# Layer 2 attention: the step loop's instructions in source order instead of a scheduler's, and the block end's rstd one piece later

## The chip, the cores and the metric

The kernel runs on one core of one Trainium2 chip, in float32 throughout. The metric is the device time of one execution in microseconds (us), lower being better. The profile is of one execution, taken by the hardware profiler; engines are named as its page names them: PE (matmul), PEld (weight load), DVE (VectorE), ACT (ScalarE), POOL (GpSimd), SP (the queue that issues most DMAs).

## The reference, cut to what matters

The program is a network of four layers on an image of 2 x 64 x 64 positions with 128 channels. Only the attention of layer 2 is touched here. It sees the image as 2 sequences (batches) of L = 4096 tokens; `t` is the residual, `_ln_t` a layer norm without weights.

```python
q = silu(x @ Wq + bq); k = silu(x @ Wk + bk); v = silu(x @ Wv + bv)
u = x @ Wu + bu                                   # 256 wide
pos_attn = einsum('nm,bmd->bnd', rel, v)          # rel is a Toeplitz matrix of pos_w
scores = einsum('bhnd,bhmd->bhnm', qh, kh) / sqrt(hd)     # 4 heads of 32
scores = where(causal, scores * scores, 0.0)
self_attn = einsum('bhnm,bhmd->bhnd', silu(scores), vh)
a = concatenate([self_attn, pos_attn], axis=-1)
a = (a - mean(a)) * rsqrt(var(a) + 1e-3) * ln_gamma + ln_beta
out = relu(u * a @ Wf + bf) + x
t = t + out                                       # x here is _ln_t(t)
```

There is no softmax: a score is squared, masked by causality and put through Silu.

## The kernel before

The kernel is written on a layer that tracks tiles and dependences. After the program is traced, a scheduler decides in which order each engine gets its instructions, by a cost model of its own; each engine then takes its queue strictly in that order, and semaphores hold an instruction until its inputs are there and its output buffer is free. The order in the source is therefore only a wish unless a region is marked as scheduled by hand.

`layer2_attn` first loads and prepares weights: the Toeplitz table `toe` (L1042 and L1043), the folded weights `wuy` and `buy` (`l2_folded`). The two sequences are then cut into 16 blocks of 512 queries, in the order 7, 0, 6, 1, 5, 2, 4, 3 for each batch, a long one and a short one in turn, since by causality block `qb` has `4 * qb + 4` tiles of 128 keys. The innermost unit is a *step*: one block and one key tile. There are 288 steps. The last four steps of each block are diagonal: they are masked by `tri`, and have 512, 384, 256 and 128 live query columns.

One step, in source order, does this. `scores` (L1301) multiplies the four heads, two heads a pair, into two score tiles of 128 x 1024 in PSUM; the pool holds two such tiles, so each is overwritten by the next step. The first pair goes to ACT, which squares it into an `es` tile (L1315), and on a diagonal step DVE masks that tile (L1318). The second pair goes to DVE, which scales it (L1328, with L1324 for the masked part), and POOL multiplies it by itself (L1331). Then come `silu(at - 1, 2)`, the Silu (L1338) of the first pair of the step before, `silu(at - 2, 3)`, the Silu of the second pair of two steps before, and `values(at - 3)` (L1352), the product of scores and values of three steps before, summed in one PSUM bank `av` over the block. At a block's end `av` is copied to `selfT` (L1363).

All other work of the layer is written as generators, cut into *pieces* by `yield`, in a table of jobs with a number of pieces each; after each step as many pieces are run as make the table finish in time (`left`, `due`). A piece may also be forced earlier, by `finish`, where something needs it. The jobs:

- `norm_stats`: the statistics (L1089, L1090) of a batch's 32 token tiles, and their rstd.
- `keys`: `transposed` (four normalises on DVE, L153, four transposes on PE, L1108, a copy on DVE, L1110, and for some an add on POOL, L1113), the key projection and its Silu (L1125, L1126), the value projection, its add and its Silu (L1130, L1138, L1141).
- `prepare`: the same `transposed` for the queries of the next block, the query projection and its Silu (L1180, L1181), and the projection `u`, four matmuls and adds (L1187, L1190). Before its first piece it finishes the output of three blocks before.
- `rest`: sums of the values on DVE (L1150), a matmul and a copy.
- `positions`: the Toeplitz product (L1202), one group of four matmuls for a key tile, then an add (L1214).
- `join`: transposes of `selfT` (L1229), a copy into `a` (L1232), the layer norm's statistics and rstd (`ln_stats`), and four products with `u` (L1236).
- `output`: eight transposes (L1251), two copies (L1252), sixteen matmul records (L1258), four multiply-adds that use the rstd (L1268), and the residual add (L1274).

The rstd (`rstd`) is one add on DVE (L95), one Sqrt on ACT (L97) and four small operations on DVE (L99 to L103). [...] ACT loads a table before and after. All the small PSUM tiles of these jobs share one tag, `misc`, with two buffers.

Of the kernel before, what the change touches and what calls it, by code (L numbers as in the profile page):

```python
# [8 lines left out]
F32 = mybir.dt.float32  # L9
# [5 lines left out]
P = 128  # L15
# [23 lines left out]
class Net:  # L39
# [969 lines left out]
    def layer2_attn(self):  # L1009
# [3 lines left out]
        nc, tc, ins = self.nc, self.tc, self.ins  # L1013
        pos_w = ins["L2_attn_pos_rev"]
        with ExitStack() as st:
# [46 lines left out]
            queries, cats, selfs, rs = {}, {}, {}, {}  # L1062
            jobs = {}

            def add(key, pieces, gen, first=False):
                if first:
                    rest = dict(jobs)
                    jobs.clear()
                    jobs[key] = [pieces, gen]
                    jobs.update(rest)  # L1070
                else:
                    jobs[key] = [pieces, gen]
# [7 lines left out]
            def finish(key):  # L1080
                while key in jobs:
                    piece(key)


            def norm_stats(b):
                mv = self.small.tile([P, NC, 2], F32, tag="l2mv", name=f"l2mv{b}", bufs=2)
                for n in range(NC):
                    s6 = self.small.tile([P, 6], F32, tag="lst", name=f"l2st{b}_{n}")
                    nc.vector.bn_stats(s6, self.x[:, b * NC + n, :])  # L1089
                    nc.vector.bn_aggr(mv[:, n, :], s6)  # L1090
                    if n % 4 == 3:
                        yield
                r = self.small.tile([P, NC], F32, tag="l2r", name=f"l2rs{b}", bufs=2)
                self.rstd(r, mv[:, :, 1], 1e-5, NC)
                kTs[b] = {}
                vs[b] = ap.tile([P, NC, C], F32, tag="v", name=f"l2v{b}")
                stats[b] = mv, r
# [18 lines left out]
            def keys(b, g, add_back=False):  # L1116
                finish(("stats", b))
                v = vs[b]
                slot = g if b == 0 else (8 + g if g < 4 else 11 - g)
                kT = ap.tile([P, 512], F32, tag=f"kT{slot}", name=f"l2kT{b}_{g}", bufs=1)  # L1120
                kTs[b][g] = kT
                xT = transposed(b, g, "k", add_back)
                yield
                pk = ps.tile([P, 512], F32, tag="misc", name=f"l2pk{b}_{g}")
                nc.tensor.matmul(pk, lhsT=wk, rhs=xT, start=True, stop=True)  # L1125
                nc.scalar.activation(kT, pk, AF.Silu, bias=bk)  # L1126
                yield
                pv = ps.tile([P, 4, C], F32, tag="misc", name=f"l2pv{b}_{g}")
                for i in range(4):
                    nc.tensor.matmul(  # L1130
                        pv[:, i, :],
                        lhsT=xT[:, i * P : (i + 1) * P],
                        rhs=wv,
                        start=True,
                        stop=True,
                    )
                part = v[:, 4 * g : 4 * g + 4, :]
                nc.vector.tensor_tensor(  # L1138
                    part, pv, bv.unsqueeze(1).broadcast_to([P, 4, C]), ALU.add
                )  # L1140
                nc.scalar.activation(part, part, AF.Silu)  # L1141
                yield
# [78 lines left out]
            def join(b, qb, i):  # L1221

                finish(("prepare", i))
                finish(("pos", i))
                a, u = cats[i], queries[i][1]
                t = f"{b}_{qb}"
                pt = ps.tile([P, 4, C], F32, tag="misc", name=f"l2st{t}")
                for j in range(4):
                    nc.tensor.transpose(  # L1229
                        pt[:, j, :], selfs[i][:, j * P : (j + 1) * P], self.ident  # L1230
                    )
                nc.vector.tensor_copy(a[:, :, :C], pt)  # L1232
                mv, r = self.ln_stats(a, 4, 1e-3, f"l2o{t}")
                rs[i] = r
                for j in range(4):
                    nc.vector.scalar_tensor_tensor(  # L1236
                        a[:, j, :], a[:, j, :], mv[:, j, 0:1], u[:, j, : 2 * C],
                        ALU.subtract, ALU.mult,
                    )
                yield  # L1240
                yield

            def output(b, qb, i):
                finish(("join", i))
                a = cats[i]
                t = f"{b}_{qb}"
                aT = ap.tile([P, 2, 512], F32, tag="aT", name=f"l2aT{t}", bufs=1)
                for k in range(2):
                    pa = ps.tile([P, 4, P], F32, tag="misc", name=f"l2pa{t}_{k}")
                    for j in range(4):  # L1250
                        nc.tensor.transpose(pa[:, j, :], a[:, j, k * C : (k + 1) * C], self.ident)  # L1251
                    nc.vector.tensor_copy(aT[:, k, :], pa.rearrange("p i q -> p (i q)"))  # L1252
                    yield
                yield
                po = ps.tile([P, 4, C], F32, tag="misc", name=f"l2po{t}")
                for j in range(4):
                    for k in range(2):
                        nc.tensor.matmul(  # L1258
                            po[:, j, :],
                            lhsT=aT[:, k, j * P : (j + 1) * P],  # L1260
                            rhs=wf[:, k, :],
                            start=(k == 0),
                            stop=(k == 1),
                        )
                o = ap.tile([P, 4, C], F32, tag="o", name=f"l2o{t}", bufs=1)
                y = queries[i][1]
                for j in range(4):
                    nc.vector.scalar_tensor_tensor(  # L1268
                        o[:, j, :], po[:, j, :], rs[i][:, j : j + 1], y[:, j, 2 * C :],
                        ALU.mult, ALU.add,  # L1270
                    )
                n0 = b * NC + 4 * qb
                xs = self.x[:, n0 : n0 + 4, :].rearrange("p i c -> p (i c)")
                nc.vector.scalar_tensor_tensor(  # L1274
                    xs, o.rearrange("p i c -> p (i c)"), 0.0, xs, ALU.max, ALU.add
                )
                yield
# [64 lines left out]
            def values(at):  # L1342
                if not 0 <= at < len(steps):
                    return
                (i, k, off), es = steps[at][:2]
                b, qb = order[i]
                last = k == 4 * qb + 3
                if k == 0:
                    avs[i] = ps.tile([P, 512], F32, tag="av", name=f"l2av{b}_{qb}", bufs=1)
                for h in range(NH):  # L1350
                    hs = slice(h * HD, (h + 1) * HD)
                    nc.tensor.matmul(  # L1352
                        avs[i][hs, off:],
                        lhsT=vs[b][:, k, hs],
                        rhs=es[h // 2][:, h % 2, off:],
                        start=(k == 0),
                        stop=last,
                    )
                if last:
                    if i >= 2:  # L1360
                        finish(("join", i - 2))
                    selfs[i] = ap.tile([P, 512], F32, tag="selfT", name=f"l2sT{b}_{qb}")
                    nc.vector.tensor_copy(selfs[i], avs[i])  # L1363
                    add(("join", i), 2, join(b, qb, i))
                    add(("out", i), 4, output(b, qb, i))

            add(("stats", 0), 8, norm_stats(0))
            add(("keys", 0, 0), 3, keys(0, 0))
            add(("prepare", 0), 4, prepare(0, 7, 0, add_back=False))
# [516 lines left out]
```

## Time and profile before

| what | value |
|---|---|
| time, median of 3 runs | 5103.84 us (5092.13 to 5111.22) |
| the profiled execution | 5117.86 us |
| its span, first to last instruction | 5116.1 us |
| mean granted TensorE clock | 0.901 |
| busy: PE, PEld, DVE | 89%, 40%, 56% of the span |
| busy: ACT, POOL | 47%, 12% of the span |
| layer 2 attention, first Square to last | 2173.2 to 3397.0 us |
| busy from 2300 to 2500 us: PE, DVE, ACT, POOL | 182.29, 97.73, 130.67, 76.88 of 200 us |

How to read it: busy time is the union of an engine's instructions. A line of the waits names an engine, a line of the source and a tile, what ended the wait, then the total in us, the number of waits and the longest. A line of a timeline has start and length in us, engine, line, operation, output and inputs, shapes and the count of instructions merged into it; in brackets stands the idle time of that engine just before, and what ended it. Each float32 matmul of the source shows as two records.

### The profile page before, as it was taken

What the parts mean: (1) busy time and instruction counts of PE and PEld (TensorE: products, weight loads), DVE (VectorE), ACT (ScalarE), POOL (GpSimd) and SP (SyncE); (2) the same over time, 40 slices, a digit from 0 to 9 for tenths busy, and PEclk for the clock granted to TensorE, in tenths of its full rate; (3) what the DMA queues carried; (4) which work ended last, traced back from release to release, by engine and by line L of the source; (5) the groups of instructions that cost most, each with busy time, mean ns of one, the idle gap of its engine ahead of it and who ended that gap; (6) DMA issues with size and microseconds to landing.
All of it is one profiled execution on the core that took longest, in us unless ns stands there. A gap on an engine that the chain in (4) does not pass through costs nothing.

```text
span 5116.1 us, 69030 instructions
## 1 busy us (share of the span) xinstructions
PE 4573.2 (89%) x28099; PEld 2063.1 (40%) x28099; DVE 2866.2 (56%) x4880; ACT 2396.9 (47%) x2773; POOL 637.6 (12%) x386
## 2 busy tenths in 40 slices
PE   7999999999999958499889988876999999999766
PEld 6433333443333326333322222224985444444432
DVE  2567777667787788854544454453032333333477
ACT  3556666655666625176666777741013222222200
POOL 1000000000000020144334444420001000000000
PEclk7899999999999978699899999975559999999889
DMA  4232323332333300000000000020410000000000
GB/s 125 66 60 47 59 63 75 81 75 57 61 53 55 61 10 1 24 1 1 1 1 1 1 1 1 1 69 26 123 51 1 0 0 0 0 1 0 5 11 24
DMA packets 132798, 164.96 MB, mean 32 GB/s; under 512 B 13904, under 2 KB 76208, under 8 KB 131568
## 3 DMA queue, kind: packets, MB, share of 16 engines
q1 hardware_dynamic: 110560, 143.25, 13.1%
q10 hardware_dynamic: 21904, 17.12, 1.1%
q8 instruction: 225, 3.69, 0.3%
q14 instruction: 109, 0.89, 0.1%
HBM read 130.97 MB, written 29.36 MB: 31 GB/s over the span
## 4 chain that ended last, share of the span: by engine, by line
PE 74%; DVE 14%; ACT 6%; POOL 4%; issue 2%; DMA 1%; SPq 0%; DVEq 0%; POOLq 0%; ACTq 0%
PE l0sc L592 18%; PE l0o L546 9%; PE scl L1650 9%; PE oTl L1667 9%; PE l2sc L1301 4%; POOL l2es L1331 3%; PE f3ex L1824 2%; ACT l2es L1338 2%; PE l2pos L1202 2%; DVE l2es L1328 2%; PE f2po L1528 2%; PE l2av L1352 2%; PE f2ph L1502 2%; ACT l2es L1315 2%; DVE l0acc L614 2%; PE l0pw L405 2%
## 5 line engine op out<-in xcount | busy, mean ns | idle before, releaser
L614 DVE TENSOR_TENSOR l0acc<-l0acc,l0es 128x1024 f32<-128x1024 f32 x988 | 1210.0, 1225 | 540.9 <-PE l0o L546 377.4
L606 ACT ACTIVATE l0es<-l0sc 128x1024 f32<-128x1024 f32 x992 | 940.3, 1031 | 387.2 <-PE l0sc L592 386.3
L592 PE MATMUL l0sc<-l0mv,ka 64*64 64x512 f32 x8192 | 993.4, 617 | 18.8 <-ACT l0es L606 16.5
L1338 ACT ACTIVATE l2es<-l2es 128x1024 f32<-128x1024 f32 (+3 forms) x576 | 562.0, 984 | 256.8 <-POOL l2es L1331 220.5
L1675 DVE TENSOR_TENSOR accl<-accl,esl 128x1024 f32<-128x1024 f32 x240 | 294.1, 1225 | 540.7 <-ACT esl L1661 482.9
L1331 POOL TENSOR_TENSOR l2es<-l2es 128x1024 f32<-128x1024 f32 (+3 forms) x288 | 504.1, 1750 | 726.6 <-DVE l2es L1328 662.9
L592 PEld LDWEIGHTS l0sc<-l0mv,ka 64*64 64x64 f32 x8192 | 297.8, 136 | 624.3 <-issue 378.5
L1661 ACT ACTIVATE esl<-scl 128x1024 f32<-128x1024 f32 x240 | 245.5, 1023 | 550.8 <-PE scl L1650 550.8
L1328 DVE TENSOR_SCALAR l2es<-l2sc 128x1024 f32<-128x1024 f32 (+3 forms) x272 | 306.8, 1128 | 341.3 <-PE l2sc L1301 341.1
L546 PE MATMUL l0o<-l0es,l0v 128*32 128x512 f32 x3968 | 495.0, 602 | 0.0
L1301 PE MATMUL l2sc<-l2q,l2kT 32*128 32x512 f32 (+3 forms) x2304 | 405.0, 623 | 91.1 <-ACT l2es L1315 67.7
L1650 PE MATMUL scl<-l3qT,l3kT 128*128 128x512 f32 x1024 | 484.1, 595 | 1.8 <-DVE bok_l L246 1.8
L1667 PE MATMUL oTl<-esl,l3v 128*128 128x512 f32 x960 | 448.5, 592 | 0.0
L1352 PE MATMUL l2av<-l2es,l2v 128*32 128x512 f32 (+3 forms) x2304 | 308.3, 603 | 0.0
L1315 ACT ACTIVATE l2es<-l2sc 128x1024 f32<-128x1024 f32 (+3 forms) x288 | 269.6, 936 | 53.6 <-PE l2sc L1301 53.2
L1650 PEld LDWEIGHTS scl<-l3qT,l3kT 128*128 128x128 f32 x1024 | 192.8, 191 | 233.2 <-issue 218.6
L1202 PE MATMUL l2pos<-l2v,toe 128*32 128x512 f32 (+3 forms) x2304 | 277.2, 572 | 0.0
L1667 PEld LDWEIGHTS oTl<-esl,l3v 128*128 128x128 f32 x960 | 182.4, 190 | 229.6 <-issue 225.8
L1301 PEld LDWEIGHTS l2sc<-l2q,l2kT 32*128 32x128 f32 x2304 | 122.8, 189 | 336.3 <-ACT l2es L1315 217.5
L868 POOL TENSOR_TENSOR l1y<-l1y,l1gb 128x1024 f32<-128x1024 f32 x8 | 20.3, 2532 | 1861.8 <-DVE l1y L862 1842.7
L546 PEld LDWEIGHTS l0o<-l0es,l0v 128*32 128x32 f32 x3968 | 106.9, 109 | 337.8 <-issue 337.8
L1832 DVE SCALAR_TENSOR_TENSOR x<-f3ex,f3wt,x 128x128 f32<-128x128 f32 x512 | 160.2, 347 | 28.5 <-PE f3ex L1824 20.0
(438 smaller groups left out, 4265.0 us busy)
## 6 DMA issues: line engine op xcount, KB each, us to landing
l0mv<-l0qd SPq DMA_DIRECT2D x128, 256.0 KB, 7.6
l0mv<-l0hd SPq DMA_DIRECT2D x256, 128.0 KB, 6.5
l0mv<-l0wd SPq DMA_DIRECT2D x128, 128.0 KB, 5.6
l0wd<-l0rw SPq DMA_DIRECT2D x4, 2048.0 KB, 6.8
l0hd<-l0hst SPq DMA_DIRECT2D x32, 256.0 KB, 2.1
f2w<-in_L_ffn_weight_dram ACTq DMA_DIRECT2D x32, 256.0 KB, 10.9
f2w<-in_L_ffn_weight_dram ACTq DMA_DIRECT2D x8, 1024.0 KB, 4.9
f2w<-in_L_ffn_weight_dram SPq DMA_DIRECT2D x8, 1024.0 KB
```

The source lines that it names most:

```text
L546: nc.tensor.matmul(o[0][at : at + HD, :], lhsT=v[:, 2 * j + s, HD * h : HD * (h + 1)], rhs=es[s][:, h, :], start=(j == 0), stop=(j == NX * ...
L592: nc.tensor.matmul(sc[64 * c : 64 * c + 64, h, :], lhsT=ka[rows, k0 : k0 + 64], rhs=mv[rows, yb, :], start=True, stop=True,)
L606: nc.scalar.activation(es, sc, AF.Exp)
L614: nc.vector.tensor_tensor(entry[5], entry[5], es, ALU.add)
L1202: nc.tensor.matmul(pos[c : c + 32, j0:, :], lhsT=toe[:, d * P + c : d * P + c + 32], rhs=v[:, n0 + j0 - d : n0 + 4 - d, :], start=(d == 0) ...
L1301: nc.tensor.matmul(sc[:, h2, off:], lhsT=kT[hs, cols], rhs=q[hs, off:], start=True, stop=True,)
L1328: nc.vector.tensor_scalar(es[:, :, lo:], sc[:, :, lo:], root, None, ALU.mult)
L1331: nc.gpsimd.tensor_tensor(part, part, part, ALU.mult)
L1338: nc.scalar.activation(e[:, :, off:], e[:, :, off:], AF.Silu)
L1352: nc.tensor.matmul(avs[i][hs, off:], lhsT=vs[b][:, k, hs], rhs=es[h // 2][:, h % 2, off:], start=(k == 0), stop=last,)
L1650: nc.tensor.matmul(sc[:, i, :], lhsT=kT[:, k * P : (k + 1) * P], rhs=qs, start=True, stop=True,)
L1667: nc.tensor.matmul(oT, lhsT=v[:, k, :], rhs=es[:, i, :], start=(k == 0), stop=(k == NC - 1),)
```

## The change

Two edits. From the point where the first jobs are added, the rest of `layer2_attn` is put under `tc.manual_schedule()`: inside it each engine receives its instructions in the order in which the source issues them. The region ends with the function. And in `join` the call of `ln_stats` is written out: the statistics come before the four products as they did, but the rstd is called after the first `yield`, so in `join`'s second piece, which was empty.

```diff
@@ in join
-                mv, r = self.ln_stats(a, 4, 1e-3, f"l2o{t}")
-                rs[i] = r
+                mv = self.small.tile([P, 4, 2], F32, tag="lmv4", name=f"mv_l2o{t}")
+                for j in range(4):
+                    s6 = self.small.tile([P, 6], F32, tag="lst", name=f"st_l2o{t}{j}")
+                    nc.vector.bn_stats(s6, a[:, j, :])
+                    nc.vector.bn_aggr(mv[:, j, :], s6)
                 for j in range(4):
                     nc.vector.scalar_tensor_tensor(
                         a[:, j, :], a[:, j, :], mv[:, j, 0:1], u[:, j, : 2 * C],
                         ALU.subtract, ALU.mult,
                     )
                 yield
+                rs[i] = self.small.tile([P, 4], F32, tag="lr4", name=f"r_l2o{t}")
+                self.rstd(rs[i], mv[:, :, 1], 1e-3, 4)
                 yield
@@ ahead of the first jobs
+            st.enter_context(tc.manual_schedule())
             add(("stats", 0), 8, norm_stats(0))
             add(("keys", 0, 0), 3, keys(0, 0))
             add(("prepare", 0), 4, prepare(0, 7, 0, add_back=False))
```

How the built programs' instructions stand shows what this moves. Before, the scheduler had put each first-pair Silu directly behind its own Square in ACT's queue, and the second pair's Silu of the same step behind that, in most steps; after, the queue is Square of a step, first-pair Silu of the step before, second-pair Silu of two steps before. PE's queue had values three steps late already and keeps that. Before, the transposes, output matmuls and query projections of a block's end were spread over the scores of the next three steps; after, transposes, output matmuls and the transposes for the next queries stand in one row between the first and the second step's scores in blocks 2 to 8 and 10 to 14 (counted from 0), in nine of these twelve with the query projection as well, and DVE's part of them likewise. Before, the statistics of batch 1 stood ahead of the loop; after, they stand in steps 14 to 18 of the first block, with a pair of table loads of their own. The other layers' instructions and SP's queue keep their order.

## The prediction

> **What bounds the kernel now.** I read the page first (groups of instructions), then the waits inside the layer-2 attention (2130 to 3440 us), then its timeline. Layer 2 attention runs from the first Square at 2173.2 us to the last at 3397.0: 1224 us for 288 steps, 24% of the span. Nothing outside it is edited. On the page two groups stand out, ACT's Silu and POOL's multiply:
>
> ```profile
> L1338 ACT ACTIVATE l2es<-l2es 128x1024 f32<-128x1024 f32 (+3 forms) x576 | 562.0, 984 | 256.8 <-POOL l2es L1331 220.5
> L1331 POOL TENSOR_TENSOR l2es<-l2es 128x1024 f32<-128x1024 f32 (+3 forms) x288 | 504.1, 1750 | 726.6 <-DVE l2es L1328 662.9
> ```
>
> After the bar is the idle time before the group and what ended it: ACT stood 220.5 us waiting for POOL. The waits give the rest:
>
> ```profile
> ACT l2es L1338 <- POOL l2es L1331: 220.5, 205, 4.2
> PEld l2sc L1301 <- ACT l2es L1315: 217.5, 179, 2.9
> ...
> DVE l2es L1318 <- ACT l2es L1315: 177.4, 61, 4.3
> ...
> ACT l2es L1338 <- DVE l2es L1318: 28.4, 59, 0.5
> ```
>
> (us, times, longest.) PE's scores wait for ACT's Square, which frees the score buffer, and ACT waits for POOL: a loop. An ordinary step, in time:
>
> ```profile
> 2407.17 1.00 ACT L1315 ACTIVATE l2es<-l2sc 128x1024 f32<-128x1024 f32 x1
> ...
> 2408.20 1.06 ACT L1338 ACTIVATE l2es<-l2es 128x1024 f32<-128x1024 f32 x1
> ...
> 2409.81 1.06 ACT L1338 ACTIVATE l2es<-l2es 128x1024 f32<-128x1024 f32 x1 [0.55 <-POOL l2es L1331]
> ...
> 2410.78 1.00 ACT L1315 ACTIVATE l2es<-l2sc 128x1024 f32<-128x1024 f32 x1
> ...
> 2411.81 2.00 ACT L1338 ACTIVATE l2es<-l2es 128x1024 f32<-128x1024 f32 x2
> ```
>
> Square to Square is 3.61 us with the wait in it and 2.94 in the next step (the Square at 2413.72): ACT's three activations back to back. So 2.95 is ACT's floor for a full step. PE's own pitch is 1.07 for scores, 0.88 for values, 0.9 for each group of positions (2405.28, 2406.35, 2407.23, 2408.22): 2.9 with one group, 3.78 with two, which the steps with two already show (3.78). The last four, diagonal, steps of a block take 5.72, 4.60, 3.48 and 2.27:
>
> ```profile
> 3386.02 0.91 PE L1301 MATMUL l2sc<-l2q,l2kT 32*128 32x384 f32 x4 [0.84 <-DVE l2es L1328]
> 3386.04 1.89 POOL L1331 TENSOR_TENSOR l2es<-l2es 128x1024 f32<-128x1024 f32 x1 [3.83 <-DVE l2es L1328]
> ...
> 3387.96 1.06 ACT L1338 ACTIVATE l2es<-l2es 128x1024 f32<-128x1024 f32 x1 [2.20 <-POOL l2es L1331]
> ...
> 3389.77 0.70 PE L1301 MATMUL l2sc<-l2q,l2kT 32*128 32x256 f32 x4 [0.99 <-ACT l2es L1315]
> ```
>
> One serial chain: scores, mask and scaling on DVE, POOL, Silu, only then the next Square. And the opening of a block, where join, output and prepare of other blocks fall due at once; here the scheduler laid the next steps' scores among them:
>
> ```profile
> 2505.47 1.06 ACT L1338 ACTIVATE l2es<-l2es 128x1024 f32<-128x1024 f32 x1 [1.27 <-POOL l2es L1331]
> ...
> 2508.55 1.28 ACT L97 ACT_TABLE_LOAD   x1
> ...
> 2514.82 1.13 DVE L1268 SCALAR_TENSOR_TENSOR l2o<-l2po,r_l2o,l2u 128x128 f32<-128x128 f32 x4 [3.37 <-PE l2po L1258]
> 2515.15 0.30 PEld L1301 LDWEIGHTS l2sc<-l2q,l2kT 32*128 32x128 f32 x4 [0.17 <-issue]
> ...
> 2518.42 1.89 POOL L1331 TENSOR_TENSOR l2es<-l2es 128x1024 f32<-128x1024 f32 x1 [7.38 <-DVE l2es L1328]
> ...
> 2518.92 1.48 DVE L153 TENSOR_SCALAR l2xn_4q<-x,l2mv,l2rs 128x128 f32<-128x128 f32 x1
> ```
>
> [...] PE is 91% busy from 2300 to 2500 us, yet ordinary steps run at 3.28 on average against a pitch of 2.9. [...] a normalise took 1.48 us beside POOL's multiply, 1.12 for four without it (2157.38). [...]
>
> **The change, part by part.** It puts every engine's instructions of the loop in the order of the source. In a step that is: PE scores, values of three steps back, then the pieces due; ACT Square, Silu of the previous step, Silu of the step before that; DVE scaling, then the pieces. POOL multiplies once a step; its add-back (1.27 at 2522.05) now stands in the step that normalised. SP issues nothing inside the loop, and its order stands. I sort before's 288 steps by what the changed order puts in them (Square to Square) and price each class.
>
> *Full steps with at most one group of positions:* 99 steps, 329 us (3.33 each). POOL is now two steps ahead of its Silu, so ACT's wait goes; next late is ACT itself, 2.95, PE at 2.9 just under it. 99 x 2.97 = 294: **-35**.
>
> *Full steps with two or more groups:* 41 steps, 147 us. PE sets 3.78 in both: **+2**.
>
> *Diagonal steps,* 14 blocks, 231 us. Lagged, from the first Square at 0: DVE masks after it (1.5), then 0.42 and 0.95 to 2.85, so PE gets the second score buffer at 2.9; values and positions to 5.3; the second pair 5.3 to 7.7, the third to 9.9, the next block's scores, Square at 11.1. Against 16.07: 5 us a block, -70. One has keys in it (+4, and the last block gains less): **-66**.
>
> *Openings,* 12 blocks, four steps each: 317 us now. In source order all these pieces stand between scores 0 and scores 1 on PE and DVE. The chain from scores at 0: scaling to 2.5, values and transposes to 2.6; copy 3.3; four statistics pairs 5.0; four products 6.8 (0.46 each); rstd with its Sqrt 8.0 (ACT has loaded the table by then; the Sqrt waits for DVE, and behind it wait only ACT's query Silu and the next Square, themselves waiting for PE); two copies 9.4; output matmuls 3.4 to 12.9; output and add 14.6; four normalises 15.7; transposes and copy 16.9; query matmul; scores 1 at **17.9**. Then 3.0 + 2.95 + 2.95 to 3.8, about 27.6 in all; the first such block 40 (nine position groups first), the last of batch 0 38 (keys first). By block, 2 to 8 and 10 to 14: 40.1, 30.1, 27.6, 31.6, 26.1, 38.3, 28.3, 27.6, 27.6, 26.1, 30.2, 26.1 = 360: **+43**. The link not seen in this order is DVE's statistic-aggregate pairs: 0.26 pitch interleaved, 0.58 if each waits for the other in full (0.41 and 0.17); I take the middle, 0.42. Unhidden throughout (all durations whole, 0.1 a hand-over), scores 1 come at 21.6; if DVE overlaps as now, at 16.5.
>
> *First 22 steps:* 108 us. Transposing keys in one step with the key projection: scaling 2.5, normalises beside POOL 4.9 (bounds 3.6 and 6.5: 1.12 for four, or held for two of POOL's multiplies), transposes 5.2, copy 5.9, matmul: 6.8, with values of v 8, v alone 3.1 to 3.6. Steps 0 to 3: 20; 4 to 11: 47; then batch 1's statistics, now in the loop and not before it, and four 1.95 us reductions load DVE: 30 for six steps; 23 for the last four. 120: **+12**. It also adds two table loads, 2.6 us, on an ACT that is waiting here.
>
> *Small:* blocks of four steps 35.5 to 37, **+1.5**; later key steps 41 to 43.5, **+2.5**; the remaining few **+5** (a 1.95 us reduction or the output matmuls alone in a step); before the loop the query chain no longer overlaps the keys', **+2**; after it two join-output chains with rstd in line, **+3.5**.
>
> *The rstd one piece later:* 16 times, same instructions. It lets the products go before ACT's Sqrt; where all pieces fall in one step it only puts 1 us of rstd ahead of the copies, counted above. Alone I price it at nothing: ACT's work covers it; uncovered, 1 us x 13.
>
> Sum: -35 + 2 - 66 + 43 + 12 + 1.5 + 2.5 + 5 + 2 + 3.5 = **-29.5**. The profiled execution took 5117.9 (span 5116.1 and 1.8 around it), 14 over the median of 5103.8; the difference carries over: 5117.9 - 29.5 = 5088.4 for it, 5103.8 - 29.5 = **5074** for the median.
>
> **Rivals.** *(1) Openings decide, slower.* PE, ACT and POOL idle while one chain passes through DVE. For it: 7.38 us of POOL idle there already, and all of join, output, prepare now in one step. Against: the durations above. Twelve openings and one short block: each us more is 13 us. At 17.9 + 29.5 / 13 = 20.2 the gain is gone, at 22.1 it is 0.5% slower; with 24, 13 x 6.1 = 79 more: 5153. *(2) Openings overlap as well as before* (DVE's pairs and copies interleave at their short pitches, normalises meet no POOL): 43 and 9 of the 12 are not paid: 5103.8 - 29.5 - 52 = 5022. *(3) PE takes half the gain:* its weight loads and clock hold full steps at 3.15 and diagonals at 12.5 a block, as the 91% suggests: 18 + 20 less to gain, 5112, no change that shows. Against: steps of 2.95 exist already. That the edit does nothing is out: the order differs on every engine.
>
> **Numbers.** Half a per cent (25.5 us) is about what a measurement of this kernel tells from no change. Forecast (-5 to -50) 0.47, of which 0.27 lies past -25.5; rival 2: 0.22; rival 3: 0.15; rival 1: 0.16. Faster 0.27 + 0.22 = 0.49, same 0.20 + 0.15 = 0.35, slower 0.16. The range leaves out about 0.08 below (half of rival 2 is under its mean) and 0.12 above: 5020 to 5122.
>
> **What would show it.** ACT's wait for POOL down from 220 to under 30 us; ordinary steps at 2.95; diagonals near 11 a block; one step of 17 to 20 us at each opening with ACT waiting for PE's query matmul. Wrong if openings exceed 21, if ordinary steps stay above 3.2, or if DVE rather than ACT ends the waits.

## The result, and the profile after

The changed kernel takes 5182.88 us (median of 4 runs, 5175.5 to 5183.82) against 5102.02 for the kernel before on the same chip: a ratio of 1.0156, 95% interval 1.0134 to 1.0177. It is slower by 1.6%; the forecast was 5074. The profiled execution took 5183.82 (span 5182.0), 66 more than that of before (the medians are 81 apart; the step times below are read from the two profiled executions); the granted clock over the span fell from 0.901 to 0.885.

The lag of the Silus behind their Squares came as forecast. On the page the Silus no longer wait at all (idle before the group 0.1 us, was 256.8):

```profile
L1336 POOL TENSOR_TENSOR l2es<-l2es 128x1024 f32<-128x1024 f32 (+3 forms) x288 | 505.0, 1753 | 647.4 <-DVE l2es L1333 553.6
...
L1343 ACT ACTIVATE l2es<-l2es 128x1024 f32<-128x1024 f32 (+3 forms) x576 | 533.3, 977 | 0.1
```

(Lines moved by five: Square is now L1320, Silu L1343, scores L1306, DVE's scaling L1333, the mask L1323.) What took its place is in the waits of the changed kernel's layer-2 attention (2130 to 3520 us; total, times, longest):

```profile
ACT l2es L1320 <- PE l2sc L1306: 227.6, 141, 11.7
...
ACT l2q L1181 <- PE l2pq L1180: 107.5, 12, 10.5
...
PEld l2sc L1306 <- ACT l2es L1320: 92.1, 109, 1.5
...
PEld l2pa L1256 <- DVE l2a L1239: 64.7, 62, 5.1
...
ACT l2kT L1126 <- PE l2pk L1125: 55.4, 13, 6.3
```

ACT now waits for PE, 9 us at a time on average at the query projections and 4 us at the key projections, and PE waits there for DVE. PE's wait for ACT's Square fell from 217.5 to 92.1.

The steps (first Square to first Square), sorted as in the prediction, in us; the last two columns are experiments told below:

| class | before | forecast | after | extra matmuls | DVE free |
|---|---|---|---|---|---|
| full, at most one position group (99) | 329.2 | 294 | 299.7 | 299.5 | 295.1 |
| full, two or more (41) | 147.3 | 149 | 149.9 | 149.9 | 150.3 |
| diagonal (56) | 230.9 | 165 | 178.9 | 179.9 | 170.4 |
| openings (48) | 317.1 | 360 | 390.0 | 352.4 | 320.4 |
| first 22 | 108.0 | 120 | 144.9 | 126.0 | 98.9 |
| four-step blocks (8) | 35.5 | 37 | 48.6 | 45.8 | 38.0 |
| later key steps (10) | 41.1 | 43.5 | 49.5 | 45.8 | 35.8 |
| rest (4) | 14.9 | 20 | 24.7 | 24.5 | 20.0 |
| loop | 1223.9 | 1188.5 | 1286.2 | 1223.8 | 1128.9 |

The first three classes gained 79 us of the forecast 99; the other five lost 141 where 64 was forecast. Here is one step of the first block with a key group in it, from the changed kernel's timeline (start, duration, engine):

```profile
2197.21 1.01 ACT L1320 ACTIVATE l2es<-l2sc 128x1024 f32<-128x1024 f32 x1
...
2198.29 2.68 DVE L153 TENSOR_SCALAR l2xn_3k<-x,l2mv,l2rs 128x128 f32<-128x128 f32 x4
...
2198.68 0.33 PE L1108 MATMUL l2t_3k<-ident,l2xn_3k 128*128 128x128 f32 x1 [0.70 <-DVE l2xn_3k L153]
...
2200.51 0.99 PE L1108 MATMUL l2t_3k<-ident,l2xn_3k 128*128 128x128 f32 x3 [1.50 <-DVE l2xn_3k L153]
2201.54 0.69 DVE L1110 COPY l2xT_3k<-l2t_3k 128x512 f32<-128x512 f32 x1 [0.57 <-PE l2t_3k L1108]
...
2202.28 2.08 PE L1125 MATMUL l2pk<-l2xT_3k,wk 128*128 128x512 f32 x2 [0.78 <-DVE l2xT_3k L1110]
...
2204.29 2.09 PE L1306 MATMUL l2sc<-l2q,l2kT 32*128 32x512 f32 x8
...
2206.41 1.03 ACT L1320 ACTIVATE l2es<-l2sc 128x1024 f32<-128x1024 f32 x1 [1.33 <-PE l2sc L1306]
...
2208.78 1.14 PE L1306 MATMUL l2sc<-l2q,l2kT 32*128 32x512 f32 x8
```

Square to Square is 9.20 us. Up to the projection, 5.07 us after the Square, it goes nearly as priced: the copy ends 6.4 us after the start of this step's scores (2195.84), where the estimate had 5.9. But then the projection takes 2.08 and the scores 2.09, where the same groups of matmuls take 1.13 and 1.14 elsewhere; the next scores, at 2208.78, are back at 1.14. The granted clock was halved in between (a stretch and its length; PE, PEld, DVE, ACT, POOL busy with their instructions; then the granted clock, the DMA share and GB/s):

```profile
2196.90:2200.30 3.40, 1.41 (x13) 0.30 (x9) 3.15 (x3) 3.21 (x4) 2.08 (x2) 1.00 0.00 0
2200.40:2207.10 6.70, 5.80 (x17) 1.76 (x21) 1.82 (x5) 1.37 (x2) 0.00 (x0) 0.50 0.00 0
2207.20:2213.90 6.70, 4.49 (x35) 1.86 (x27) 5.07 (x7) 5.56 (x7) 3.82 (x2) 1.00 0.00 0
```

In the 3.4 us ahead of the fall PE was busy for 1.4, with values and one transpose, and no single wait was longer than 1.5. The other three transposes, the projection and the scores then ran at half clock. The same in the opening step of the fifth block:

```profile
2550.58 1.03 ACT L1320 ACTIVATE l2es<-l2sc 128x1024 f32<-128x1024 f32 x1 [1.54 <-PE l2sc L1306]
...
2551.95 0.69 DVE L1232 COPY l2a<-l2st 128x512 f32<-128x512 f32 x1
...
2552.68 0.43 DVE L1236 BATCH_NORM_STATS2 st_l2o<-l2a 128x6 f32<-128x256 f32 x1
...
2554.82 1.64 DVE L1239 SCALAR_TENSOR_TENSOR l2a<-l2a,mv_l2o,l2u 128x256 f32<-128x256 f32 x4
...
2557.50 1.28 DVE L1257 COPY l2aT<-l2pa 128x512 f32<-128x512 f32 x2
...
2558.24 3.95 PE L1263 MATMUL l2po<-wf,l2aT 128*128 128x128 f32 x16 [0.40 <-DVE l2aT L1257]
...
2564.00 1.11 DVE L153 TENSOR_SCALAR l2xn_2q<-x,l2mv,l2rs 128x128 f32<-128x128 f32 x4
...
2566.28 2.08 PE L1180 MATMUL l2pq<-l2xT_2q,wq 128*128 128x512 f32 x2 [0.78 <-DVE l2xT_2q L1110]
...
2568.28 2.09 PE L1306 MATMUL l2sc<-l2q,l2kT 32*128 32x512 f32 x8
...
2570.47 1.02 ACT L1320 ACTIVATE l2es<-l2sc 128x1024 f32<-128x1024 f32 x1 [1.39 <-PE l2sc L1306]
```

19.9 us, one serial chain through DVE as the prediction drew it: the copy ahead of the query projection ends 16.8 us after the start of the scores (2549.40), priced at 16.9. Then projection and scores are again at double length, and the output matmuls (3.95) stand in half clock too. The lengths go with the granted clock: 2.08 at 0.50, 1.13 at 1.00. PE need not be idle throughout for it to fall. In the clock records of the changed kernel's trace each stretch at one clock within the loop is 3.41 us long or a multiple of it. The clock fell 36 times in the loop, each time behind 3.4 us in which PE was busy for 1.8 or less, and, on the same beat of 3.41 us, only one other stretch at full clock with as little work (1.79) was not followed by a fall; in the kernel before it fell 24 times, 23 of them behind 3.4 us with 2.2 or less, and nine other stretches with as little were not followed by a fall. So the halved clock isn't new: it held for some 140 us of the loop before and for 311 after (granted clock over the loop 0.94 and 0.88). Counted over stretches, kernel before first, then the changed one:

```profile
2200.00:2300.00 100.00, 90.15 (x548) 30.85 (x551) 55.03 (x68) 72.34 (x77) 46.69 (x26) 0.93 0.00 1
2500.00:2700.00 200.00, 178.96 (x1246) 60.79 (x1242) 103.21 (x184) 143.79 (x156) 84.10 (x49) 0.94 0.00 1
```

```profile
2200.00:2300.00 100.00, 76.89 (x327) 27.67 (x327) 59.54 (x123) 50.92 (x58) 28.29 (x16) 0.69 0.00 0
...
2500.00:2700.00 200.00, 169.20 (x1128) 65.45 (x1132) 101.94 (x180) 120.68 (x139) 74.49 (x44) 0.85 0.00 1
```

In the first block PE executed 327 matmul records in 100 us where it was 548, and still shows 77% busy: a slow clock looks like work.

### The profile page after: what moved, and what is told of

The parts are those of the page before. It is cut to its first block, busy times and chain, and to the rows that moved or that the text cites. A ratio compares the mean times of both kernels' runs of the same rounds, so it can differ in the third digit from the quotient of the medians.

```text
span 5182.0 us, 69067 instructions
## 1 busy us (share of the span) xinstructions
PE 4597.3 (89%) x28099; PEld 2109.5 (41%) x28099; DVE 2901.2 (56%) x4880; ACT 2366.3 (46%) x2775; POOL 638.5 (12%) x386
## 4 chain that ended last, share of the span: by engine, by line
PE 81%; DVE 14%; ACT 2%; issue 1%; DMA 1%; POOL 0%; SPq 0%; DVEq 0%; ACTq 0%; POOLq 0%
PE l0sc L592 17%; PE scl L1656 9%; PE l0o L546 9%; PE oTl L1673 8%; PE l2sc L1306 6%; PE l2av L1357 5%; PE l2pos L1202 4%; PE f3ex L1830 2%; PE f2po L1534 2%; PE f2ph L1508 2%; DVE l0acc L614 2%; PE l0pw L405 2%; PE l0ph L420 1%; PE l2po L1263 1%; PE l2pu L1187 1%
## 5 line engine op out<-in xcount | busy, mean ns | idle before, releaser
L592 PE MATMUL l0sc<-l0mv,ka 64*64 64x512 f32 x8192 | 993.6, 617 | 18.8 <-ACT l0es L606 16.5
L1343 ACT ACTIVATE l2es<-l2es 128x1024 f32<-128x1024 f32 (+3 forms) x576 | 533.3, 977 | 0.1
L1333 DVE TENSOR_SCALAR l2es<-l2sc 128x1024 f32<-128x1024 f32 (+3 forms) x272 | 306.8, 1128 | 397.0 <-PE l2sc L1306 392.7
L1320 ACT ACTIVATE l2es<-l2sc 128x1024 f32<-128x1024 f32 (+3 forms) x288 | 274.1, 952 | 233.7 <-PE l2sc L1306 227.6
L1306 PE MATMUL l2sc<-l2q,l2kT 32*128 32x512 f32 (+3 forms) x2304 | 359.7, 651 | 6.2 <-DVE l2es L1333 3.6
L1306 PEld LDWEIGHTS l2sc<-l2q,l2kT 32*128 32x128 f32 x2304 | 109.8, 195 | 235.7 <-ACT l2es L1320 92.1
L1830 PE MATMUL f3ex<-ew,f3xnT 128*128 128x512 f32 x256 | 128.6, 624 | 54.4 <-DVE x L1838 54.4
```

What stands on the lines that cost most here:

```text
L592: nc.tensor.matmul(sc[64 * c : 64 * c + 64, h, :], lhsT=ka[rows, k0 : k0 + 64], rhs=mv[rows, yb, :], start=True, stop=True,)
L1306: nc.tensor.matmul(sc[:, h2, off:], lhsT=kT[hs, cols], rhs=q[hs, off:], start=True, stop=True,)
L1333: nc.vector.tensor_scalar(es[:, :, lo:], sc[:, :, lo:], root, None, ALU.mult)
L1343: nc.scalar.activation(e[:, :, off:], e[:, :, off:], AF.Silu)
```

## The experiments

Two questions: is the halved clock a cause with a price of its own, and what in the source order makes the stretches serial? Diffs are against the changed kernel; ratios are to runs of the kernel before on the same chip, with 95% intervals.

**The two parts apart.** First the rstd's move without the order, then the order without the move:

```diff
-            st.enter_context(tc.manual_schedule())
```

> Only the rstd of a block's end is moved one piece later; the loop keeps the scheduler's order. My theory: the move costs nothing, since it is the same instructions; 5102, within 10 of the kernel before. Rival (the moved rstd stalls DVE and ACT at every block end, 13 times 1 to 2 us, and is a part of the loss): 5115 to 5130.

Measured: 5101.83, ratio 0.9988 (0.9975 to 1.0002).

```diff
-                mv = self.small.tile([P, 4, 2], F32, tag="lmv4", name=f"mv_l2o{t}")
...
+                mv, r = self.ln_stats(a, 4, 1e-3, f"l2o{t}")
+                rs[i] = r
```

> Only the order of issue is changed; the rstd stays before the products, as in the kernel before. My theory: the whole loss is in the order, so this is as slow as the full change, 5183 within 6. Rival (the two parts only hurt together, or the rstd's place matters once the order is fixed): 5165 or less, or 5195 or more.

Measured: 5187.46, ratio 1.016 (1.0128 to 1.0193). The rstd costs nothing, as priced; the loss is all in the order.

**The order from the second block on.**

```diff
-            st.enter_context(tc.manual_schedule())
...
+                if i == 1:
+                    st.enter_context(tc.manual_schedule())
```

> The source order is entered only at the second block: block 0 with its eight key groups, and what stands ahead of the loop, keep the scheduler's order. Block 0 took 180.1 us in source order and 146.8 before. My theory: the loss is spread, half of it in block 0: 5183 - 35 = 5148, still 0.9% above the kernel before. Rival A (block 0 is the whole loss, the rest breaks even): 5100 to 5115. Rival B (block 0 is not the place, its time only moves): 5175 to 5190.

Measured: 5147.96, ratio 1.0076 (1.0047 to 1.0106). The first block holds some 35 us of the loss (36 by the loops' lengths), the rest is spread: both rivals are out.

**PE kept at work where it waits.**

```diff
+            def warm(pt, cols, n=1):
+                for _ in range(n):
+                    nc.tensor.matmul(
+                        pt[:, :cols], lhsT=self.ident, rhs=toe[:, :cols], start=True, stop=True
+                    )
...
                 pt = ps.tile([P, 512], F32, tag="misc", name=f"l2t{t}")
+                if steps:
+                    warm(pt, 512, 2)
...
                 pk = ps.tile([P, 512], F32, tag="misc", name=f"l2pk{b}_{g}")
+                if steps:
+                    warm(pk, 256)
...
                     pa = ps.tile([P, 4, P], F32, tag="misc", name=f"l2pa{t}_{k}")
+                    if k == 0:
+                        warm(pa.rearrange("p i q -> p (i q)"), 512, 3)
```

(and one of 256 ahead of the query projection.)

> The full change with extra matmuls on PE, whose results are overwritten by the next real ones in the same PSUM tile, where PE waits for DVE in the key and opening steps: two of 512 columns ahead of each set of four transposes, three ahead of the block-end transposes, one of 256 ahead of the key and query projections. They add work and take no wait away. My theory (the serial stretches leave PE idle, the granted clock drops, and the next matmuls take twice as long): key steps fall from 9.3 to about 7, opening steps from 19.9 to about 18, the mean clock in the first block rises from 0.75 to over 0.9; 5183 - 55 = 5128, anything from 5115 to 5150. Rival (the clock plays no role; the chain through DVE alone sets the steps): no step gets shorter, and the extra matmuls cost up to 1 us in each of 30 steps, 5183 to 5210.

Measured: 5118.3, ratio 1.0018 (1.0009 to 1.0027): some 120 us of useless PE work (in the loop, groups of L1102) made the kernel 65 us faster than the change. The same key step in its timeline, extra matmuls on L1102:

```profile
2196.85 1.98 PE L1102 MATMUL l2t_3k<-toe,ident 128*128 128x512 f32 x4
...
2199.46 0.84 PE L1117 MATMUL l2t_3k<-ident,l2xn_3k 128*128 128x128 f32 x3 [0.51 <-DVE l2xn_3k L153]
...
2200.13 0.60 PE L1102 MATMUL l2pk<-toe,ident 128*128 128x256 f32 x2
...
2201.08 1.12 PE L1136 MATMUL l2pk<-l2xT_3k,wk 128*128 128x512 f32 x2 [0.35 <-DVE l2xT_3k L1119]
...
2202.14 1.14 PE L1321 MATMUL l2sc<-l2q,l2kT 32*128 32x512 f32 x8
```

The chain up to the projection is as long as in the change (4.93 us after the Square at 2196.15), projection and scores are back at 1.12 and 1.14, and the step takes 7.16 instead of 9.20. The fifth block's opening takes 16.5. The granted clock in the same two stretches:

```profile
2200.00:2300.00 100.00, 88.50 (x438) 31.64 (x437) 67.79 (x132) 59.62 (x67) 34.83 (x19) 0.90 0.00 1
...
2500.00:2700.00 200.00, 187.30 (x1254) 70.16 (x1246) 107.78 (x192) 131.03 (x152) 80.76 (x48) 0.97 0.00 1
```

So the clock is a cause by itself, worth 62 us in the loop (1286.2 to 1223.8), net of what the extra matmuls themselves cost; they bring the loop's granted clock from 0.88 to 0.97, above the 0.94 of the kernel before. It isn't the first cause: the stretch in which PE waits is.

**Which engine's order makes it serial.** The order by source was fixed for some engines only:

```diff
-            st.enter_context(tc.manual_schedule())
+            st.enter_context(tc.manual_schedule(engines={mybir.EngineType.Activation}))
```

> Source order on ACT alone; PE, DVE and POOL are ordered by the scheduler again. Only in ACT's order does the lag of the Silus need to be fixed. My theory: ACT's order itself carries the loss, since the query's or key's Silu stands ahead of the next Square on ACT, so that PE can run at most the first pair of the next scores ahead of the pieces; the statistics interleave and PE has a little more to do: 5155, between 5140 and 5175. Rival (PE's and DVE's fixed orders are what makes the openings serial): the openings overlap as before while the lag stays, 5050 or less.

Measured: 5017.12, ratio 0.9825 (0.9799 to 0.9851). My expectation failed and the rival held: ACT's order costs nothing, and with PE, DVE and POOL left to the scheduler the change is a gain of 1.8%. Then ACT with PE, and ACT with DVE:

> Source order on ACT and PE; DVE and POOL are ordered by the scheduler. PE's and ACT's orders are exactly those of the full change, so this changes DVE's order and what hangs on it. With source order on ACT alone (5017) DVE normalises a key group two groups ahead of its transposes. My theory now: DVE's fixed order is the loss, since it puts each normalise straight ahead of the transpose that PE then waits for: 5035, from 5015 to 5060. Rival (PE's fixed order, with no scores between the pieces, is the loss): 5130 or more.

Measured: 5016.96, ratio 0.9829 (0.9803 to 0.9855).

> Source order on ACT and DVE; PE is ordered by the scheduler, DVE's order is exactly that of the full change. My theory: PE can't run ahead of a DVE that normalises late, so the key steps stay at 8 to 9 us and the clock still drops: 5160, from 5130 to 5185. Rival (PE's order is the loss): 5050 or less.

Measured: 5170.32, ratio 1.0136 (1.0111 to 1.016). PE's order is in the first of the two exactly that of the change, and nothing of the loss is left; DVE's is in the second exactly that of the change, and nearly all of it is there. DVE's order is the loss. (POOL's order came out as in the change in the second run too; so the place of POOL's few add-backs is not told apart from DVE's order.) A key step with DVE free (order of ACT and PE by source):

```profile
2196.84 0.66 PE L1108 MATMUL l2t_4k<-ident,l2xn_4k 128*128 128x128 f32 x4
...
2197.53 0.69 DVE L1110 COPY l2xT_4k<-l2t_4k 128x512 f32<-128x512 f32 x1 [0.23 <-PE l2t_4k L1108]
2198.14 1.98 DVE L153 TENSOR_SCALAR l2xn_6k<-x,l2mv,l2rs 128x128 f32<-128x128 f32 x4
...
2198.28 1.13 PE L1125 MATMUL l2pk<-l2xT_4k,wk 128*128 128x512 f32 x2 [0.78 <-DVE l2xT_4k L1110]
...
2200.23 1.14 PE L1306 MATMUL l2sc<-l2q,l2kT 32*128 32x512 f32 x8
```

While PE is at group 4, DVE normalises group 6: the scheduler had been running DVE two groups ahead, so that PE's transposes found their input ready and PE had one wait of 0.78 us ahead of the projection, where the change has three in a row (0.70, 1.50, 0.78). The source, read as an order, says to normalise straight ahead of the transpose.

**Only the normalises earlier,** all engines in source order:

```diff
+                if kind == "k" and b == 0 and g < 7:
+                    normal(b, g + 1, kind)
                 return xT
...
                 if i >= 3:
+                    normal(b, qb, "q")
                     finish(("out", i - 3))
```

(`normal` holds the four normalises of `transposed`, which then skips them.)

> Source order on every engine as in the full change, but the source has the normalises earlier: those of block 0's next key group straight after the transposes of the group before, those of a query ahead of join and output instead of behind them. My theory (the place of the normalises on DVE is most of the loss of the first block and a part of the openings'; with them early PE doesn't fall idle and its clock holds): key steps of block 0 from 9.3 to about 5, openings 1.5 shorter but still serial through join and output: 5183 - 45 - 18 = 5120, from 5100 to 5140. Rival (no single place matters; only a scheduler's interleaving of all of DVE's work helps): 5165 or more.

Measured: 5133.04, ratio 1.0059 (1.0038 to 1.008), 50 us less than the change. Key steps of the first block fall from some 9 to some 4.4 us, its first 22 steps from 144.9 to 107.8, as fast as before; openings only from 390.0 to 379.1. So the place of the normalises is the loss in the first 22 steps, and little of the openings'.

**The order only between the openings.**

```diff
+                    if k == (22 if i == 0 else 4):
+                        hand.enter_context(tc.manual_schedule())
                     scores(i, k)
...
+                hand.close()
```

> Source order only between the openings: from the fifth step of each block to its end, in block 0 from the 23rd step; the openings and the first 22 steps are left to the scheduler. My theory: the ordinary and diagonal steps keep their gain (30 and 52 us), the openings their old time: 5109 - 70 = 5040, from 5020 to 5070. Rival (the openings' old overlap took its work out of the steps beside them, so that fixing those steps makes the openings longer): 5090 or more.

Measured: 5035.07, ratio 0.9867 (0.984 to 0.9895). The lag's gain is there for the taking; openings took 286 against 317.

**The source itself spread out.** Normalises, transposes and projection become pieces of their own (one `yield` more in `transposed`, one in `join`), a step takes its pieces from different jobs, and join and output go as soon as nothing holds them, not when the next query forces them:

```diff
                     while due > 0 and jobs:
-                        piece(next(iter(jobs)))
-                        due -= 1
+                        for key in sorted(jobs, key=lambda key: key not in begun):
+                            if due > 0 and key in jobs and not held(key):
...
+                                piece(key)
+                                due -= 1
...
-                    add(("join", i), 2, join(b, qb, i))
-                    add(("out", i), 4, output(b, qb, i))
+                    add(("out", i), 3, output(b, qb, i), first=True)
+                    add(("join", i), 3, join(b, qb, i), first=True)
```

(`held` says which jobs wait for another; `o` shares the buffers of `xn`, three in all.)

> Source order on every engine, but the source's order is changed: normalises, transposes, projection and values of a key group or query are pieces of their own, a step takes its pieces from different jobs, join and output go as soon as they can and are no longer forced into the next block's first step. No step holds more than one DVE-to-PE hand-over of a job. My theory (the order by source is sound, the serial bundles in one step are the loss, with the clock as their second price): no step over 10 us, clock above 0.95 in the loop, and the lag's gain stays; loop 1130 against 1224 before, 5109 - 90 = 5020, anything from 4990 to 5060. Rival (a fixed order on DVE is the loss wherever the pieces stand, since scaling now waits behind them): the steps with pieces take 5 us instead of 3, 100 x 2 us, no gain: 5090 to 5180.

Measured: 4983.0, ratio 0.9764 (0.9739 to 0.979); loop 1096 us, no step over 8.6, clock 0.97 and 0.98 in the two stretches above. That is better than expected (4990 to 5060). A fixed order on DVE isn't bad as such; my reading, argued from this run and the one with earlier normalises, is that the order has to keep a producer ahead of its consumer. The same source with ACT's order alone, and with none:

> The pieces spread over the steps as in the spread version (4983), but source order on ACT alone. If the spread leaves nothing for a scheduler to mend, the same, 4983 within 12. If DVE's fixed order still costs where a normalise stands ahead of a scaling, 4955 to 4970. If the scheduler undoes the spread, 5000 or more.

Measured: 4973.44, ratio 0.9744 (0.9719 to 0.977), the lowest median here, but within what was expected for "the same": the two intervals overlap, and the 10 us to the spread in full order aren't shown to be a difference.

> The spread version's source with no fixed order anywhere, so that the scheduler puts the Silus where it did before. My theory: the lag's gain (some 80 us on ordinary and diagonal steps) goes and only the split pieces' gain stays: 5070, from 5040 to 5100. Rival (the spread is the whole gain and the order adds nothing): 4990 or less.

Measured: 5059.25, ratio 0.9918 (0.9893 to 0.9942). Without ACT's order the diagonal steps go back from 189 to 229 us, the size of before. So ACT's fixed order brings 86 us on this source, and the spread brings some 45 without it.

## Why the prediction was wrong, point by point

- **Full steps, -35:** -29.5 (3.03 each for 2.97). Right; ACT's wait for POOL went. **Two or more groups, +2:** +2.6. **Rstd, 0:** nothing that shows.
- **Diagonal steps, -66:** -52. Mis-sized: 12.1 us in most blocks for 11.1, and 19.0 and 15.3 in two whose last steps hold other work. In most blocks the mask, 0.42 in my chain, met POOL's multiply, which now runs two steps ahead of its Silu; here it takes 1.38:

```profile
2637.80 1.90 POOL L1336 TENSOR_TENSOR l2es<-l2es 128x1024 f32<-128x1024 f32 x1 [2.57 <-PE l2sc L1306]
...
2638.59 1.38 DVE L1323 TENSOR_TENSOR l2es<-l2es,tri 128x256 f32<-128x256 f32 x1 [0.96 <-ACT l2es L1320]
```

  The mask ends just after POOL's multiply, at 2639.97 against 2639.70, and the scaling that frees the next score buffer stands behind it; that this is the whole of the 1 us a block is argued from the timeline, no run took it apart. That an operation of DVE can take longer beside POOL's multiply, which I had used for the normalises, was left out here: of the changed kernel's 64 masks the 27 clear of a multiply took 0.42 or 0.43, the 37 that overlap one 0.49 to 1.47. The scaling of a full tile, which reads PSUM, kept its duration (1.22 to 1.23 where it overlaps a multiply, 1.21 to 1.23 where not).
- **Openings, +43:** +73, the step that failed first. The drawn chain was right, and its price high if anything: with the clock held, 352 for the 360 forecast. The missing term is the clock: "query matmul; scores 1 at 17.9" took PE's full-clock durations, where the chain itself had let the clock fall; the projection and the scores took 1 us more each. Holding the clock is worth 390.0 - 352.4 = 38 us here. The trace of before had shown it:

```profile
2509.40 2.08 PE L1301 MATMUL l2sc<-l2q,l2kT 32*128 32x512 f32 x4
2511.40 3.38 PE L1258 MATMUL l2po<-wf,l2aT 128*128 128x128 f32 x16
```

  Four score matmuls take 2.08 there, in a stretch of half clock (0.50 from 2507.5 to 2514.2), and 1.13 at 2515.15, with the clock back at 1.00. The chain's 3.4 for the output matmuls was taken there too, at a granted clock of 0.58 (in the seven blocks of that trace that have them at 1.00, PE spends 2.05 to 2.32 on them), so the prediction had the clock in one link without knowing it and not in the next. Smaller: the statistics pairs took 0.53 each for the 0.42 priced.
- **First 22 steps, +12:** +37. The same term: 144.9 - 126.0 = 19 us. The key projections and scores were priced at full clock. With the clock held, 126 for the 120 forecast.
- **Four-step blocks, +1.5:** +13. Mis-sorted: the second of them holds an opening of its own (a step of 16.95). **Later key steps, +2.5:** +8.4, 3.7 of it the clock; the rest is the chain with the normalises at 2.7 beside POOL. **The remaining few, +5:** +9.8, most of it one step that waits behind the four reductions (9.6).
- **Outside the loop, +5.5:** 65.9 - 62.3 = +3.6.

Together the clock is 62 of the 95 us between forecast (-29.5) and result (+65.9), the diagonal steps 14, the four-step blocks' chain some 9. Rival 3 spoke of the clock, but put it where PE is busy, in full steps, where it stayed at its best (1.4 us at half of 300); it struck where PE waits. Its 12.5 us for a block's diagonal steps came near the 12.1 measured, for another reason. Rival 1 had the sign, and its place: openings too long. The openings came out 2.5 us each over their price, just past the 2.3 at which it had the gain gone; the loss beyond that was paid in other places, the first 22 steps above all. Rival 2's 5022 is close to what the kernel takes when DVE isn't ordered by source (5017), in part by luck, as it had the diagonal steps 5 us too low and the first 22 steps 12 us too high: the overlap I took for a property of the operations was the scheduler's work on DVE's order, which the change undoes. The mark "DVE rather than ACT ends the waits" was the right one to watch.

What stays open: which of DVE's moves shortens the openings with DVE free (14.7 us in the fifth block; statistics staggered, copies ahead of the rest of rstd, the query normalised a block ahead) was not taken apart, only that the normalises alone give 11 of the 70 us.

## What to carry to other kernels

A switch to source order takes away every run-ahead that the scheduler had found, on each engine: before flipping it, look on the producing engine for work that stood well ahead of its consumer, and fix the order only on the engine that needs it. In the changed kernel's loop 36 of the 37 stretches of 3.4 us at full clock with 1.8 us of PE work or less were followed by the halved clock, and the full clock came back most often 6.8 us after the fall (21 of 36). When a change opens such a stretch, an estimate from this case is double length (2.08 for 1.13) for the matmuls behind it until the clock is back; that was two thirds of the error here (62 of 95 us). And look whether a duration taken from the old trace was itself measured at half clock. PE's busy share doesn't show it (77% in 100 us at a clock of 0.69): read the granted clock by stretches, and compare the duration of one known group.

## What the runs showed of the hardware that was not expected

- The clock was halved though PE was not idle throughout: in the changed kernel every one of the 36 falls in the loop came behind 3.4 us with 0.02 to 1.8 us of PE work, in the key step with 1.4 and waits of 0.70 and 1.50 only. Groups of 1.13 and 1.14 us then took 2.08 and 2.09; with two matmuls of 512 columns ahead of the transposes and one of 256 ahead of the projection the two groups were back at 1.12 and 1.14.
- The statistic and its aggregate on DVE: a pair every 0.53 us where each waits for the one before, 0.39 where the next statistic is put between (with DVE free).
